# An adaLN mixture-of-experts kernel: a branch hint ahead of the code behind the expert blocks, one product fewer at its start, and the last tile's output in two halves

## The chip, the cores and the metric

The kernel runs on one core of a Trainium2 chip. The metric is the device time of one execution in microseconds; three executions of the kernel before gave 560.17, 560.28 and 561.66 us, with a median of 560.28 us. One further execution was taken under the hardware profiler, and all rows quoted below come from it. Its own device time is 562.46 us, of which the span from the first to the last instruction is 560.6 us.

The engines are named as the profile names them: PE is the matrix engine (PEld are its weight loads), DVE the vector engine, ACT the scalar engine, POOL the GpSimd engine, SP the engine that here only issues DMAs. A letter q behind a name (PEldq, SPq) marks an engine's sequencer, the part that fetches instructions, waits on semaphores and takes branches. L1157 is line 1157 of the kernel's source before the change.

## What is computed

There are 4 batches of 512 rows with 512 columns, in float32. A conditioning layer comes first, then a mixture-of-experts feed-forward layer with 32 experts, 4 of them for each row and at most 512 slots in each expert, and a shared expert beside it. Cut to its core:

```
q_emb = relu(cond @ W3 + b3)
hidden = relu(((512 * x + sum_rows(x)) * q_emb) @ W2 + b2)          # per batch
h = rmsnorm(hidden) * norm_w
scores = softmax(h @ gate_w.T);  top 4 experts, their weights scaled to sum 1
for each expert e, its rows in order, the first 512 of them:        # C = 512
    routed[row] += weight * ((silu(rows @ w13_gate) * (rows @ w13_up)) @ w2[e])
shared = (silu(h @ shared_gate) * (h @ shared_up)) @ shared_down
out = x + hidden + routed + shared
```

A row past an expert's 512 slots is not simply left out by the reference: its index is clipped when the results are read back, so that it receives the result of the expert's last slot, times its own weight. The kernel keeps these "rows of last slots" apart, as is told below.

## The kernel before

The kernel records every operation through a small layer (`op`, line 113): each operation goes to the end of its engine's list, and the layer works out which semaphores it has to wait for from the tiles that it reads and writes. So the order of the Python calls is the order on each engine, and an engine never takes an operation ahead of one that waits.

**The stages.** First the conditioning layer, the gate and the sorting of rows into experts (to about 124 us). Then a long run of blocks: a block is two units of 64 rows that belong to one expert each, and for each the rows are gathered, multiplied by the two weight matrices of their expert, and added into a buffer in DRAM by POOL's scattering DMAs (L1108). How many blocks there are depends on the data, between 16 (`NMIN`) and 80 (`NMAX`); here there are 61. The code of all 80 blocks is written out one behind the other, and ahead of each block from the sixteenth on every engine but SP compares the block's number with the count and either goes on or branches away (L1385).

**The endings.** The branch goes to one of 65 pieces of code, `ending(i)`, one for each possible count: it finishes the one or two blocks still in flight and does a part of the shared expert of batch 1 in between: on PE two halves of a product into `TX[1]` (L880), the transposes and the second product of the last block (L541, L1180), and then `s_half(1, 1, sg_sb, TX[0])`, four products into the bank `TX[0]` (L548). Each ending closes with an unconditional branch (L1393) to code that is there once on each engine, called the rest here (`PE_rest` and so on). In memory the 80 blocks come first, then the 65 endings in order, then the rest.

**The rest** is the shared expert of batches 1, 0, 2 and 3 (batch 0's was computed in front of the blocks) and the sum of all parts. Its order on PE, as recorded:

- `s_half(1, 1, su_sb, GU[1])`: four products (L548); the first waits until ACT and DVE have closed their endings
- four transposes of `over`, the weights of the rows past the slots, into `D[0]` (L541); ACT copies them to `overT` (L1346)
- `down(j)` for the tiles 1, 2, 3, 0 of batch 1 (L1319): two products each, from `t_act` and `sd_sb` into the bank `BK[j]`, where BK is `[D[0], D[1], TA[0], TA[1]]`; they wait for DVE's product of silu and up (`s_mult`, L897)
- `products(2, 0)`: the gate half into `TX[0]`, the up half into `TX[1]`; ACT's silu (L894), DVE's product (L897)
- the rows of last slots: two tiles `lrow[0]` and `lrow[1]` of 32 rows and 512 columns, read from the two DRAM buffers, are multiplied by `copies`, a matrix that repeats the 32 rows four times, and summed in the bank `GU[1]`; ACT copies the sum to `lrows` (L1353)
- then for batches 1, 0, 2 and 3 in turn the shared expert's products, `past(b, ...)` (L1312: four products of 32 rows that add the rows of last slots) and `down`, and for each tile `result(t)`: DVE adds the bank to the sums in `y_sb` (L1330) and SP writes the tile of 128 rows and 512 columns to the output.

SP reads the sums back at the start of the rest (`yin`, L1288: `lrow[0]`, `lrow[1]`, then eight loads of 1 MB), when all scattering DMAs have landed, and POOL adds the two halves of the sums in place (`both`, L1326), four tiles for each batch in the order 1, 0, 2, 3. Two of the lines that the change moves:

```
    op("PE", matmuls([(GU[1][:], copies[:].rearrange("e t f -> e (t f)"), lrow[i][:]) for i in range(2)]),
       r=[copies[:], lrow[0][:], lrow[1][:]], w=[GU[1][:]])
```

Of the kernel before, what the change touches and what calls it, by code (L numbers as in the profile page):

```python
# [11 lines left out]
ALU = mybir.AluOpType  # L12
AX = mybir.AxisListType

P = 128
# [9 lines left out]
class Program:  # L25
# [87 lines left out]
    def op(self, eng, fn, r=(), w=(), lane=None, signal=True, also=(), key=None):  # L113
        need = {}

        def depend(token):
            key, val = token
            need[key] = max(need.get(key, 0), val)

        for token in also:  # L120
            depend(token)
        for x in r:
            for c in self.cells(x):
                if c in self.writer:
                    t = self.writer[c]
                    if not (eng == "PE" and self.owner[t[0]] == "PE"):
                        depend(t)
        for x in w:
            for c in self.cells(x):
                if c in self.writer:  # L130
                    t = self.writer[c]
                    if not (eng == "PE" and self.owner[t[0]] == "PE"):
                        depend(t)
                for t in self.readers.get(c, {}).items():
                    if not (eng == "PE" and self.owner[t[0]] == "PE"):
                        depend(t)
        if lane is not None:
            ring = self.lanes[lane]
            key = ring[self.lane_next[lane]]
            self.lane_next[lane] = (self.lane_next[lane] + 1) % len(ring)  # L140
            if self.count[key]:
                depend((key, self.count[key]))
            self.count[key] += 16
            token, step = (key, self.count[key]), 16
        elif signal:
            key = key or self.own[eng]
            self.count[key] += 1
            token, step = (key, self.count[key]), 1
        else:
            token, step = None, 0  # L150
        waits = self.learn(eng, need)
        if token:
            self.seen[token] = dict(self.known[eng])
            for x in r:
                for c in self.cells(x):
                    self.readers.setdefault(c, {})[token[0]] = token[1]
            for x in w:
                for c in self.cells(x):
                    self.writer[c] = token
                    self.readers.pop(c, None)  # L160
        else:
            assert not w
        self.out[eng].append((waits, fn, token and token[0], step))
        return token
# [43 lines left out]
def adaln_moe_kernel(nc, stack, x, xt, cond, W3, b3, W2, b2, norm_w, gate_w, wx, sg, su, sd, out):  # L208
    B, S, H = x.shape
    Q = cond.shape[1]  # L210
    E = gate_w.shape[0]
# [4 lines left out]
    NT = T // P  # L216
    TB = S // P
# [23 lines left out]
    op = k.op  # L241
# [4 lines left out]
    out_rows = out.rearrange("b (t p) h -> (b t) p h", p=P)  # L246
# [16 lines left out]
    sg_sb = keep("sg_sb", [P, HC, I], F32)  # L263
    su_sb = keep("su_sb", [P, HC, I], F32)
    sd_sb = keep("sd_sb", [P, IC, H], F32)
# [9 lines left out]
    last = keep("last", [P, 2, NCOL], F32)  # L275
# [110 lines left out]
    t_act = k.sbuf("t_act", [P, IC, S], F32, k.place[hT[0].name][1])  # L386
    t_silu = [k.sbuf(f"t_silu{i}", [P, S], F32, at) for i, at in enumerate((after_up2, k.place[hT[0].name][1] + 4096))]
    y_sb = [k.sbuf(f"y{i}", [P, NT, H], F32, ring_at + i * NT * H * 4) for i in range(2)]
    overT = k.sbuf("overT", [P, B, P], F32, ring_at + 2 * NT * H * 4)
    lrow = [k.sbuf(f"lrow{i}", [E, H], F32, ring_at + (2 * NT + 1 + i) * H * 4) for i in range(2)]  # L390
    lrows = k.sbuf("lrows", [P, H], F32, ring_at + (2 * NT + 3) * H * 4)
    copies = k.sbuf("copies", [E, TB, E], F32, ring_at + (2 * NT + 4) * H * 4)
    assert 2 * NT + 5 <= NBUF * WROW // H

    TX = [k.bank(f"TX{i}", i) for i in range(2)]
    GU = [k.bank(f"GU{i}", 2 + i) for i in range(2)]
# [17 lines left out]
    def dma(eng, out_ap, in_ap, lane, r=(), w=()):  # L414
        return op(eng, lambda e: e.dma_start(out=out_ap, in_=in_ap, allow_slow_non_contiguous=True), r=r, w=w, lane=lane)
# [129 lines left out]
    def matmuls(terms):  # L545
        def fn(e):
            for n, (o, lt, rh) in enumerate(terms):
                last = e.matmul(o, lhsT=lt, rhs=rh, start=(n == 0), stop=(n == len(terms) - 1))  # L548
            return last
        return fn  # L550
# [20 lines left out]
    for c in range(QC):  # L571
        op("PE", transposes([(TA[0][:, c * 8 : c * 8 + B], cond_sb[:, c * P : (c + 1) * P], B)]),
           r=[cond_sb[:], ident[:]], w=[TA[0][:]])
# [4 lines left out]
    for c in range(HC):  # L578
        bank = (TX + GU)[c]
        op("PE", matmuls([(bank[:, 0:B], W3_sb[:, kc, c * P : (c + 1) * P], condT[:, kc, :]) for kc in range(QC)]),  # L580
           r=[W3_sb[:], condT[:]], w=[bank[:]])
# [236 lines left out]
    for t in range(NT):  # L818

        g, i = divmod(t - 5, TB)  # L820
# [29 lines left out]
        b, i = divmod(t, TB)  # L850
# [38 lines left out]
    def s_half(b, i, w_sb, pg, key=None):  # L889
        op("PE", matmuls([(pg[:], w_sb[:, c, i * P : (i + 1) * P], hT[b][:, c, :]) for c in range(HC)]),  # L890
           r=[w_sb[:]] + [("hT", b * TB + j) for j in range(TB)], w=[pg[:]], key=key)
# [22 lines left out]
    for e in range(FREE):  # L914
# [22 lines left out]
       r=[cumj[:], ones[:]], w=[TA[1][:]])  # L937
# [6 lines left out]
       w=[active[:]])  # L944
# [4 lines left out]
       r=[ranks[:], before[:], till[:], active[:]], w=[TA[1][:]])  # L949
    op("PE", matmuls([(TA[0][0:1, 4 * NCOL : 4 * NCOL + E], active[:, i : i + 1], upto[:]) for i in range(2)]),  # L950
       r=[active[:], upto[:]], w=[TA[0][:]])
# [13 lines left out]
    for i in range(2):  # L965
        op("DVE", lambda e, i=i: e.tensor_scalar(place[i][:], iota_bk[:], rank[:, i : i + 1], None, ALU.is_equal),
           r=[iota_bk[:], rank[:]], w=[place[i][:]])
    op("DVE", lambda e: e.tensor_tensor(places12[:], place[0][:], place[1][:], ALU.add), r=[place[0][:], place[1][:]],
       w=[places12[:]])
    for t in (12, 13):  # L970
# [9 lines left out]
       r=[scol[:], units], w=[TA[0][:]])  # L980
    op("PE", lambda e: e.matmul(TA[0][0:1, 2 * NCOL : 4 * NCOL], lhsT=ecol[:], rhs=units, start=True, stop=True),
       r=[ecol[:], units], w=[TA[0][:]])
# [21 lines left out]
    for t in range(12, NT):  # L1004
# [11 lines left out]
       r=[empty[:], spare[:], GU[0][:]], w=[idxf[:]])  # L1016
# [14 lines left out]
       r=[needs[:]], w=[tab[:]])  # L1031
# [6 lines left out]
       w=[rel[:]])  # L1038
# [261 lines left out]
    def products(b, i, gate=True):  # L1300
        if gate:
            s_half(b, i, sg_sb, (TX if i == 0 else GU)[0])
        s_half(b, i, su_sb, (TX if i == 0 else GU)[1])
        s_silu_of((TX if i == 0 else GU)[0], t_silu[i][:])
        s_mult(t_silu[i][:], (TX if i == 0 else GU)[1], t_act[:, i, :])

    BK = [D[0], D[1], TA[0], TA[1]]

    def past(b, start, stop):

        for j in range(TB):
            op("PE", lambda e, j=j: e.matmul(BK[j][:], lhsT=overT[j * E : (j + 1) * E, b, :],  # L1312
                                             rhs=lrows[j * E : (j + 1) * E, :], start=start, stop=stop),
               r=[overT[:], lrows[:]], w=[BK[j][:]])

    def down(j, start, stop):
        def fn(e):
            for i in range(IC):
                last = e.matmul(BK[j][:], lhsT=t_act[:, i, j * P : (j + 1) * P], rhs=sd_sb[:, i, :],  # L1319
                                start=start and i == 0, stop=stop and i == IC - 1)  # L1320
            return last
        op("PE", fn, r=[t_act[:], sd_sb[:]], w=[BK[j][:]])

    def both(t):
        a, b = y_sb[0][:, t, :], y_sb[1][:, t, :]
        op("POOL", lambda e: e.tensor_tensor(a, a, b, ALU.add), r=[a, b], w=[a])  # L1326

    def result(t):
        a, po = y_sb[0][:, t, :], BK[t % TB]
        op("DVE", lambda e: e.tensor_tensor(a, a, po[:], ALU.add), r=[a, po[:]], w=[a])  # L1330
        dma("SP", out_rows[t], a, "ost", r=[a])

    for b in order:
        sums_in(b)
# [7 lines left out]
       w=[copies[:]])  # L1342
    for g in range(B):
        op("PE", transposes([(D[0][:, g * P : (g + 1) * P], over[:, g * TB : (g + 1) * TB, :].rearrange("p t e -> p (t e)"),
                              P)]), r=[over[:], ident[:]], w=[D[0][:]])
    op("ACT", lambda e: e.copy(overT[:], D[0][:].rearrange("p (b t) -> p b t", b=B)), r=[D[0][:]], w=[overT[:]])  # L1346
    for j in (1, 2, 3, 0):
        down(j, True, False)
    products(2, 0)

    op("PE", matmuls([(GU[1][:], copies[:].rearrange("e t f -> e (t f)"), lrow[i][:]) for i in range(2)]),
       r=[copies[:], lrow[0][:], lrow[1][:]], w=[GU[1][:]])
    op("ACT", lambda e: e.copy(lrows[:], GU[1][:]), r=[GU[1][:]], w=[lrows[:]])  # L1353
    s_half(2, 1, sg_sb, GU[0])
    past(1, False, True)
    for j in range(TB):
        result(TB + j)
# [8 lines left out]
        result(2 * TB + j)  # L1366
    products(3, 0, False)
    products(3, 1)
    past(3, True, False)
    for j in range(TB):  # L1370
        down(j, False, True)
        result(3 * TB + j)
    k.wait("SP", k.lane_tokens("ost"))


    def writer(eng):
        def fn(e):
            k.emit(e, before_loop[eng])
            if eng != "SP":
                n = k.reg["n" + eng]  # L1380
                root, parents = nc.cur_bb, {}
                for i in range(NMAX):
                    if i >= NMIN:
                        parents[i] = nc.cur_bb
                        e.br_lt(n, i + 1, on_true=f"{eng}_end{i}", on_false=f"{eng}_blk{i}")  # L1385
                        nc.switch_bb(f"{eng}_blk{i}", parent=parents[i])
                    k.emit(e, bodies[i][eng])
                parents[NMAX] = nc.cur_bb
                e.br(f"{eng}_end{NMAX}")
                for i in range(NMIN, NMAX + 1):  # L1390
                    nc.switch_bb(f"{eng}_end{i}", parent=parents[i])
                    k.emit(e, endings[i][eng])
                    e.br(f"{eng}_rest")  # L1393
                nc.switch_bb(f"{eng}_rest", parent=root)
            k.emit(e, after_loop[eng])
        return fn
# [45 lines left out]
```

## Time and profile before

| what | value |
|---|---|
| three executions | 560.17, 560.28, 561.66 us |
| the profiled execution | 562.46 us |
| its span | 560.6 us |
| PE busy | 549.7 us, 98% of the span, 2518 products |
| DVE, ACT, POOL busy | 287.2, 220.8, 287.4 us |
| the 61 blocks, up to the branch to the ending | about 124 to 483 us |
| the ending on PE | 483.9 to 493.3 us |
| the rest on PE | 495.5 to 557.3 us |
| the last tile: DVE's sum, then its DMA | 557.40 us, 558.12 us |

How to read it: a group of instructions on one engine is shown with its start, its length, its line, what it writes and reads, and how often it occurs; a float32 product of 512 columns shows as two matrix instructions, each started 0.43 us after the one before when PE is kept supplied, so four products are "x8". Idle time ahead of a group stands in brackets with what ended it; "issue" says that no semaphore in the profile accounts for it. The mean clock granted to PE is shown as a share of full speed.

### The profile page before, as it was taken

How to read it: one execution, taken by the hardware profiler on the slowest of the kernel's cores; microseconds unless marked ns; L12 is line 12 of the kernel's file. 1: busy time of each engine (PE TensorE's matmuls, PEld its weight loads, DVE VectorE, ACT ScalarE, POOL GpSimd, SP SyncE). 2: the span in 40 equal slices, each digit the busy share in tenths (PEclk: the TensorE clock that was granted, in tenths of full speed). 3: DMA queues.
4: the chain of work that ended last, by engine and by line, in shares of the span. 5: the costliest groups of instructions: out<-in, count | busy, mean ns of one | idle time of the engine just before them, and what ended most of it. 6: DMA issues, size and time to landing. Idle time of an engine off the chain costs nothing.

```text
span 560.6 us, 7813 instructions
## 1 busy us (share of the span) xinstructions
PE 549.7 (98%) x2518; PEld 237.1 (42%) x2518; DVE 287.2 (51%) x807; ACT 220.8 (39%) x428; POOL 287.4 (51%) x237
## 2 busy tenths in 40 slices
PE   8999999999999999999999999999999999989997
PEld 5455665443433333433334433334333334334342
DVE  3569998956455444555444554444554445210422
ACT  3648666823334433434333344333344334300000
POOL 1102200235766666576667776756766766415800
PEclk9999999999999999999999999999999999989999
DMA  8886888956686968797997889989999655439921
GB/s 300 286 324 239 283 337 279 360 174 190 111 198 112 238 147 197 197 238 180 250 260 185 236 242 267 238 230 251 222 250 248 113 103 92 67 56 381 343 77 75
DMA packets 49198, 120.21 MB, mean 214 GB/s; under 512 B 8404, under 2 KB 9432, under 8 KB 48056
## 3 DMA queue, kind: packets, MB, share of 16 engines
q1 hardware_dynamic: 32896, 83.24, 43.9%
q0 software_dynamic: 15040, 34.39, 31.2%
q10 hardware_dynamic: 1208, 1.92, 1.0%
q8 instruction: 26, 0.43, 0.3%
q14 instruction: 28, 0.23, 0.1%
HBM read 89.36 MB, written 34.36 MB: 221 GB/s over the span
## 4 chain that ended last, share of the span: by engine, by line
PE 92%; DVE 3%; ACT 2%; issue 1%; DMA 1%; POOL 0%; SPq 0%; DVEq 0%; ACTq 0%
PE GU L1157 37%; PE D L1180 20%; PE D L548 7%; PE TX L541 5%; PE TX L548 5%; PE GU L548 4%; PE TA L541 4%; PE D L1319 2%; PE TA L1319 2%; PE TX L880 2%; PE TA L548 1%; DMA z<-in_xt_dram 1%; PE D L598 1%; PE D L558 1%; PE D L1312 1%
## 5 line engine op out<-in xcount | busy, mean ns | idle before, releaser
L1108 POOL DMA_INDIRECT y_rows<-eo,sidx x122 | 180.4, 1479 | 102.8 <-DMA y_rows<-eo,sidx 34.7
L1157 PE MATMUL GU<-ring,xT 128*64 x488 | 214.5, 592 | 0.6 <-issue 0.6
L1157 PE MATMUL GU<-up,xT 128*64 128x512 f32 x488 | 214.5, 592 | 0.0
L1157 PEld LDWEIGHTS GU<-ring,xT 128*64 128x64 f32 x488 | 66.8, 137 | 139.4 <-issue 139.4
L1165 DVE TENSOR_TENSOR act<-silu,GU 128x256 f32<-128x256 f32 x61 | 25.7, 422 | 176.3 <-ACT silu L1164 143.4
L1180 PE MATMUL D<-ring,actT 128*64 x244 | 111.3, 599 | 0.2 <-issue 0.2
L1180 PE MATMUL D<-down,actT 128*64 128x512 f32 x244 | 111.3, 599 | 0.0
L1100 POOL DMA_INDIRECT rows<-h_rows,idx x66 | 70.5, 1068 | 33.6 <-issue 13.1
L1164 ACT ACTIVATE silu<-GU 128x256 f32<-128x256 f32 x61 | 23.5, 385 | 147.6 <-PE GU L1157 147.6
L1157 PEld LDWEIGHTS GU<-up,xT 128*64 128x64 f32 x488 | 66.8, 137 | 0.0
L1068 ACT COPY up<-ring 128x1024 f32 x62 | 64.3, 1037 | 5.8 <-DVE up L1068 5.5
L1184 ACT ACTIVATE eo<-D,wrow 128x512 f32<-128x512 f32 x61 | 41.9, 687 | 51.5 <-PE D L1180 42.7
L1180 PEld LDWEIGHTS D<-ring,actT 128*64 128x64 f32 x244 | 30.9, 136 | 58.0 <-issue 58.0
L548 PE MATMUL D<-W_sb,z 128*128 128x512 f32 x120 | 54.3, 595 | 0.2 <-POOL z L563 0.2
L1068 DVE COPY up<-ring 128x1024 f32 x62 | 44.7, 721 | 0.8 <-issue 0.8
L1068 DVE COPY down<-ring 128x1024 f32 x62 | 42.7, 714 | 0.1
L1096 DVE COPY xT<-TX 128x512 f32<-128x512 f32 x62 | 40.0, 686 | 4.4 <-issue 2.0
L563 POOL TENSOR_SCALAR z<-z,vs,q_sb 128x512 f32<-128x512 f32 x12 | 9.8, 816 | 55.7 <-ACT junk L554 55.6
L541 PE MATMUL TX<-ident,rows 128*128 128x128 f32 x248 | 32.3, 273 | 0.0
L1171 ACT COPY actT<-TA 128x256 f32<-128x256 f32 x61 | 22.8, 373 | 24.1 <-PE TA L541 18.1
L548 PEld LDWEIGHTS D<-W_sb,z 128*128 128x128 f32 x120 | 21.7, 190 | 22.4 <-issue 22.0
L1180 PEld LDWEIGHTS D<-down,actT 128*64 128x64 f32 x244 | 30.9, 136 | 0.0
(207 smaller groups left out, 561.2 us busy)
## 6 DMA issues: line engine op xcount, KB each, us to landing
ring<-in_L_ffn_w_dram SPq DMA_DIRECT2D x96, 384.0 KB
ring<-in_L_ffn_w_dram SPq DMA_DIRECT2D x8, 1536.0 KB
y<-y_rows SPq DMA_DIRECT2D x8, 1024.0 KB, 13.4
h_rows<-h SPq DMA_DIRECT2D x16, 256.0 KB, 4.5
y_rows<-hid SPq DMA_DIRECT2D x16, 256.0 KB, 4.1
out_dram<-y SPq DMA_DIRECT2D x16, 256.0 KB, 2.3
z<-in_xt_dram SPq DMA_DIRECT2D x14, 256.0 KB, 5.3
y_rows<-eo,sidx POOLq DMA_INDIRECT x122
```

The lines of the kernel that those rows point to most:

```text
L541: last = e.transpose(o, i, ident[:n, :n])
L548: last = e.matmul(o, lhsT=lt, rhs=rh, start=(n == 0), stop=(n == len(terms) - 1))
L1068: return e.copy(dst, src) if eng == "ACT" else e.tensor_copy(dst, src)
L1096: return op("DVE", lambda e: e.tensor_copy(xt[:], pt[:].rearrange("p (c t) -> p c t", c=HC)), r=[pt[:]], w=[xt[:]])
L1100: op("POOL", lambda e: e.indirect_dma_start(out=r[:], out_offset=None, in_=h_dram, in_offset=bass.IndirectOffsetOnAxis(ap=idx[:, i : i + 1 ...
L1108: op("POOL", lambda e, o=o, y=y, at=at: e.indirect_dma_start(out=y, out_offset=bass.IndirectOffsetOnAxis(ap=at, axis=0), in_=o, in_offset= ...
L1157: last = e.matmul(pg[h * U : (h + 1) * U, :], lhsT=xt[:, c, h * U : (h + 1) * U], rhs=w, start=(c == 0), stop=(c == HC - 1))
L1164: op("ACT", lambda e: e.activation(s, pg[:, 0:I], AF.Silu), r=[pg[:]], w=[s])
L1165: op("DVE", lambda e: e.tensor_tensor(a, s, pg[:, I : 2 * I], ALU.mult), r=[s, pg[:]], w=[a])
L1171: op("ACT", lambda e: e.copy(at[:], pt[:, 0 : IC * P].rearrange("p (c t) -> p c t", c=IC)), r=[pt[:]], w=[at[:]])
L1180: last = e.matmul(po[h * U : (h + 1) * U, :], lhsT=at[:, c, h * U : (h + 1) * U], rhs=w2, start=(c == 0), stop=(c == IC - 1))
L1184: op("ACT", lambda e: e.activation(o, po[:], AF.Copy, scale=w), r=[po[:], w], w=[o])
```

## The change

Four edits are made, all in or behind the endings.

- Each ending on PE begins with a branch hint: the place is marked at the ending's first instruction, and the unconditional branch at its end is named as the hinted one. No other engine gets one. In the instruction lists this is one instruction more in each of the 65 endings on PE.
- In the rest, the gate half of `products(2, 0)` is recorded ahead of the four `down`, so on PE it stands between the transposes of `over` and `down`.
- The two products with `copies` become one: DVE adds `lrow[1]` to `lrow[0]` first. In DVE's list the sum stands behind the product of silu and up of `products(2, 0)`, and reads two tiles in SBUF of 32 rows and 512 columns.
- The last tile of batch 3 is computed in two halves of 256 columns, the left one in `TA[1]` as before, the right one in `TX[0]`: `past`, `down`, DVE's sum and the output's DMA occur twice for it, each on 256 columns. SP issues 17 output DMAs in place of 16.

The instruction lists of the two kernels differ in nothing else.

```diff
-    def past(b, start, stop):
+    def past(b, start, stop, tiles=range(TB)):
-        for j in range(TB):
+        for j in tiles:
             op("PE", lambda e, j=j: e.matmul(BK[j][:], lhsT=overT[j * E : (j + 1) * E, b, :],
...
-    def down(j, start, stop):
+    def down(j, start, stop, f0=0, f1=H, bank=None):
+        bank = bank or BK[j]
         def fn(e):
             for i in range(IC):
-                last = e.matmul(BK[j][:], lhsT=t_act[:, i, j * P : (j + 1) * P], rhs=sd_sb[:, i, :],
+                last = e.matmul(bank[:, f0:f1], lhsT=t_act[:, i, j * P : (j + 1) * P], rhs=sd_sb[:, i, f0:f1],
                                 start=start and i == 0, stop=stop and i == IC - 1)
...
-    def result(t):
-        a, po = y_sb[0][:, t, :], BK[t % TB]
-        op("DVE", lambda e: e.tensor_tensor(a, a, po[:], ALU.add), r=[a, po[:]], w=[a])
-        dma("SP", out_rows[t], a, "ost", r=[a])
+    def result(t, f0=0, f1=H, bank=None):
+        a, po = y_sb[0][:, t, f0:f1], (bank or BK[t % TB])[:, f0:f1]
+        op("DVE", lambda e: e.tensor_tensor(a, a, po, ALU.add), r=[a, po], w=[a])
+        dma("SP", out_rows[t][:, f0:f1], a, "ost", r=[a])
...
+    s_half(2, 0, sg_sb, TX[0])
     for j in (1, 2, 3, 0):
         down(j, True, False)
-    products(2, 0)
-
-    op("PE", matmuls([(GU[1][:], copies[:].rearrange("e t f -> e (t f)"), lrow[i][:]) for i in range(2)]),
-       r=[copies[:], lrow[0][:], lrow[1][:]], w=[GU[1][:]])
+    products(2, 0, False)
+
+    op("DVE", lambda e: e.tensor_tensor(lrow[0][:], lrow[0][:], lrow[1][:], ALU.add), r=[lrow[0][:], lrow[1][:]],
+       w=[lrow[0][:]])
+    op("PE", matmuls([(GU[1][:], copies[:].rearrange("e t f -> e (t f)"), lrow[0][:])]),
+       r=[copies[:], lrow[0][:]], w=[GU[1][:]])
...
-    past(3, True, False)
-    for j in range(TB):
+    halves = ((0, H // 2, BK[TB - 1]), (H // 2, H, TX[0]))
+    past(3, True, False, range(TB - 1))
+    for f0, f1, bank in halves:
+        op("PE", lambda e, f0=f0, f1=f1, bank=bank: e.matmul(
+            bank[:, f0:f1], lhsT=overT[(TB - 1) * E : TB * E, 3, :], rhs=lrows[(TB - 1) * E : TB * E, f0:f1],
+            start=True, stop=False), r=[overT[:], lrows[:]], w=[bank[:]])
+    for j in range(TB - 1):
         down(j, False, True)
         result(3 * TB + j)
+    for f0, f1, bank in halves:
+        down(TB - 1, False, True, f0, f1, bank)
+        result(NT - 1, f0, f1, bank)
...
                 for i in range(NMIN, NMAX + 1):
                     nc.switch_bb(f"{eng}_end{i}", parent=parents[i])
+                    hint = e.mark_branch_hint_location() if eng == "PE" else None
                     k.emit(e, endings[i][eng])
-                    e.br(f"{eng}_rest")
+                    to_rest = e.br(f"{eng}_rest")
+                    if hint is not None:
+                        to_rest.branch_hint(hint)
```

## The prediction

> **What bounds the kernel now.** I read the busy shares first, then the chain of waits from 482 us on, because the change touches nothing before that.
>
> ```profile
> PE 549.7 (98%) x2518; PEld 237.1 (42%) x2518; DVE 287.2 (51%) x807; ACT 220.8 (39%) x428; POOL 287.4 (51%) x237
> ...
> 489.70 3.63 PE TX L548 x8
> 493.33 2.21 issue
> 495.54 5.40 PE GU L548 x8
> ...
> 501.06 0.68 DVE t_act L897
> 501.74 0.04 issue
> 501.78 1.98 PE D L1319 x4
> ...
> 508.92 6.87 PE TX L548 x16
> 515.78 5.54 PE GU L548 x12
> ...
> 553.86 3.45 PE TA L1319 x8
> ...
> 557.40 0.69 DVE y L1330
> ```
>
> PE sets the time. Behind the blocks its chain has three blemishes: 2.21 us of nothing at the start of the rest, a first group that takes 5.40 us where every other "x8" takes 3.4 to 3.7, and a wait for DVE's product at 501. Next I read the windows, for the clock, and the branch's own record.
>
> ```profile
> 493.50:496.90 3.40, 1.36 (x3) 0.68 (x4) 0.62 (x1) 0.46 (x1) 0.31 (x1) 1.00 0.38 51
> 496.90:500.30 3.40, 3.40 (x5) 1.31 (x4) 0.00 (x0) 0.00 (x0) 0.00 (x0) 0.50 0.02 5
> ...
> 555.00:558.40 3.40, 2.30 (x6) 0.75 (x4) 1.37 (x2) 0.00 (x0) 0.00 (x0) 1.00 0.41 154
> 558.40:560.60 2.20, 0.00 (x0) 0.00 (x0) 0.00 (x0) 0.00 (x0) 0.00 (x0) 1.00 0.32 119
> ...
> L1393 PEldq COMPARE_BRANCH  x1: 3992/3992/3992, 487.8 to 487.8; - x1
> ```
>
> The columns of the windows are length, busy time of PE, PEld, DVE, ACT, POOL, PE's granted clock, DMA share and GB/s. After a stretch in which PE was busy 1.36 of 3.40 us the clock was halved for one stretch: that is the 5.40. After 2.30 of 3.40 it was not.
>
> The branch to the rest took PE's sequencer 3.99 us, from 487.78 to 491.77. But PE still had products queued until 493.07, so **the branch itself is hidden**. In the trace's records of transfers, PE's code arrives in loads of 16,384 bytes: one runs from 489.41 to 490.35 (the branch's target), the next from 492.52 to 494.23. The rest's first instruction, a wait, is recorded at 491.84, its second at 495.53. So I read the gap thus: the rest begins at the very end of a load, and PE runs dry on the next one. A pair of blocks has 135 PE instructions in 11.91 us, and loads come every 23.0 us ((478.04 - 109.95) / 16), so a load holds about 260 instructions.
>
> **The change part by part**, against the profiled execution.
>
> *Hint, and the place of the rest.* 65 endings grow by one instruction, so the rest moves 65 instructions on, out of the end of a load, with some 195 of it left in that load: over 15 us of work, which covers the next load. With that, or with a hint that fetches early, PE goes on when the last product is issued: the eighth starts at 489.63 + 7 x 0.43 = 492.64, the next is due at 493.07 and came at 495.54. Saved: 2.4 us; 0 if the rest again meets a load's end. The cover is the 4 x 2 x 0.43 = 3.4 us of the ending's last product; without it the branch's 4.0 us would show. The hint stands where PE is already idle (483.00 to 483.91), so its price counts in full: at least the 0.05 us of another sequencer instruction (the regops of L1180 took 46 to 53 ns), at most the 4.0 us of the branch if it waits for the fetch. A hint has only to issue a request, like the first: 0.05.
>
> *The clock.* Without the gap its drop goes: 5.40 - 3.70 = 1.7 us; 0 if the new stall below brings one back.
>
> *The gate half ahead of `down`.* PE waits 0.41 us for DVE's product at 501.37; now 3.4 us of products stand there and cover it: 0.4 saved. ACT's silu comes earlier too, and nothing waits for it.
>
> *One product fewer, one sum on DVE.* Two matrix instructions go: 2 x 0.43 = 0.86 us saved. But the sum stands in DVE's list behind `products(2, 0)`'s product, and this one waits for the up half, which PE issues directly ahead of the `copies` product. Where PE went on at 515.71, it now waits: DVE's product starts at 515.89, the sum can start 0.60 later (DVE's sums of L1330 in a row: two in 1.29) and takes 0.70 (between 0.69 of L1330 and 0.75 of L611, 128x512 with both inputs in SBUF), and PE follows 0.07 later (501.73 to 501.78 for the same step): 517.26, that is 1.55 late. The sum also reads two SBUF tiles while POOL adds the halves of the sums:
>
> ```profile
> 100.69 0.97 DVE L733 SCALAR_TENSOR_TENSOR blk<-idf,blk 128x16 f32<-128x16 f32 x1
> ...
> 100.59 1.04 POOL L762 TENSOR_TENSOR over<-over,kept 128x384 f32<-128x384 f32 x1
> ...
> 510.72 4.93 POOL L1326 TENSOR_TENSOR y<-y,y 128x512 f32<-128x512 f32 x4 [16.90 <-DMA y<-y_rows]
> 516.14 4.93 POOL L1326 TENSOR_TENSOR y<-y,y 128x512 f32<-128x512 f32 x4 [0.49 <-DMA y<-y_rows]
> ```
>
> L733 with two SBUF inputs needs 0.17 us alone and took 0.97, to the end of POOL's instruction; L737 at 46.98 lost 0.38 in the same way, and then ran between two of POOL's. So the sum waits 0 to 1.27 us (one instruction of L1326); I take 0.5, between the losses 0.38 and 0.80. Together 1.55 + 0.5 - 0.86 = +1.2, from +0.6 to +2.0. Behind the `copies` product stand all further products of PE and ACT's copy to `lrows`. The loads of `lrow` land 2.2 us after 501.4, long before. On DVE `result(4)` stands behind, at 522.5 less about 2 to 4 us, while POOL's sums for it end at 515.65 and at most 0.7 later.
>
> [...]
>
> *A new clock drop.* The stall leaves PE idle about 1.55 + 0.5 + 0.1 = 2.1 us, up to 62% of 3.4, against the 60% that brought a drop and the 32% that did not: 0 to +1.7. [...]
>
> *The last tile.* DVE's last sum falls from 0.69 (L1330) to 0.42 (L1165, 128x256): 0.27. Its DMA moves half: 64 KB (lrow) land in 2.2 us, 256 KB in 2.3, so 0.1, at most 0.34 (half of a queue's 8 packets of 0.085 us). PE works as long: `past`'s fourth runs beside the other three in its own rows, and a weight load of 0.19 fits under 0.21 of a half product. SP's one issue more (0.33) stands 0.86 ahead of the last. 0.4 saved, 0.1 to 0.6.
>
> **Sum** without clock: -2.4 + 0.05 - 0.4 + 1.2 - 0.4 = -1.95. The profiled execution, 562.46, is 2.2 us above the median of 560.28, more than one drop; so I can't tell whether the median holds a drop. Where the drop is in both kernels or in neither, the median goes to 560.28 - 1.95 = **558.3**.
>
> **The cases.**
> - *Forecast, 46%*: as summed, 558.3; own range 557.4 to 559.3.
> - *The old drop goes, none comes, 28%*: -1.7 more, 556.6. For it: a gap of 2.47 us fills over half of some 3.4 us stretch at most alignments. Against it: the new stall is nearly as long.
> - *Only the new stall brings a drop, 12%*: 560.0.
> - *The change doesn't do what it says, 8%*: the branch was hidden already, and the rest's place gains nothing because another load's end lies as badly: the gap stays, 558.3 + 2.4 = 560.7.
> - *Slower, 6%*: the hint waits for its fetch at the ending's first instruction, where no product is queued. Price 4.0 us, and a drop of 1.7 behind 4.9 us of idle PE: 558.3 + 4.0 + 1.7 = 564.0. For it: the branch's record, which does wait. From a price of 2.0 on the kernel is no faster.
>
> 0.3% is 1.7 us here, about what a measurement can tell: faster is below 558.6, slower above 562.0. About two thirds of the forecast (0.30) and the second case (0.28) with a little of the others give 0.60 for faster; the slower case with the upper ends of the two before it 0.09; same 0.31. The range 556.0 to 560.6 takes the first three cases and the unknowns of the sum.
>
> **What would show it.** PE's branch at the ending's end takes far below 3.99 us, and the rest's first product follows the ending's last at once, at full clock. On the `copies` product stands an idle time of PE of 1.6 to 2.9 us, put down to DVE's sum; the sum shows above 0.75 us if POOL holds it. The wait ahead of `down` is gone. DVE's last sum takes 0.42. I am wrong if PE is idle at the ending's first product for more than 0.95 us, if the gap before the rest stays, or if the sum ends ahead of the up half.

## The result, and the profile after

Over 16 runs of each, the changed kernel has a median of 559.46 us (557.17 to 561.53) and the kernel before 560.37 us (559.50 to 563.16). The ratio is 0.9969, with a 95% interval from 0.9952 to 0.9986: about 1.7 us less by the ratio, 0.9 by the medians. The profiled execution of the changed kernel took 560.65 us, its span 558.8; the one before took 562.46, its span 560.6.

The changed kernel's runs fall into two groups by the mean granted clock that each run reports. Six runs at 1.000 have a median of 558.28 us, ten at 0.994 to 0.997 one of 560.07. One stretch of 3.41 us at half clock is 1.7 us lost, or 0.3% of the mean clock, and that is the distance of the two groups (1.8 us). Of the kernel before, 34 later runs were taken on three chips; five of them stand at 0.996 or 0.997 (two of 21, three of 11, none of two) and the rest at 0.999 or 1.000. The mean clock does not say where a stretch at half clock lies. In three of the profiles below that show 0.997 (without the hint near a load's end, the later hint, the early sum without the hint) it lies at 8.4 to 11.8 us, in the first stage, and none lies between there and the last product.

First the busy shares of the changed kernel, from the top of its page:

```profile
PE 549.1 (98%) x2522; PEld 238.4 (43%) x2522; DVE 287.9 (52%) x809; ACT 220.7 (40%) x428; POOL 287.1 (51%) x237
```

PE sets the time as it did (the counts are of matrix instructions, two for each float32 product). Next its chain of waits from the ending's last product on; the columns are start, length and what ran.

```profile
490.27 3.63 PE TX L548 x8
493.90 3.43 PE GU L548 x8
...
508.07 3.45 PE TX L548 x8
...
512.22 1.56 DVE lrow L1354
...
513.82 6.45 PE GU L548 x10
...
555.39 0.88 PE TX L1321 x4
556.27 0.02 issue
556.29 0.42 DVE y L1332
```

All three blemishes of the profile before are gone: the rest's first product starts at 493.90, the moment the ending's last ends, it takes 3.43 us where it took 5.40, and no wait for DVE stands at 501. A new one has come in their place. PE ends its last block of products at 511.52 and goes on at 513.82, behind DVE's sum of the two `lrow` tiles, and the group that follows takes 6.45 us. Ten such instructions at full clock take 4.68 (the same group in an experiment below). The windows, with the columns that the prediction names, show why:

```profile
512.00:515.40 3.40, 1.58 (x3) 0.59 (x4) 1.76 (x2) 0.42 (x1) 3.40 (x3) 1.00 1.05 389
515.40:518.90 3.50, 3.50 (x6) 1.43 (x5) 0.00 (x0) 0.16 (x1) 3.47 (x4) 0.51 1.05 388
518.90:522.30 3.40, 3.40 (x15) 1.16 (x14) 0.87 (x2) 0.60 (x1) 2.91 (x3) 1.00 1.05 387
```

PE was busy for 1.58 of 3.40 us, and in the next stretch it got half its clock. The drop lasted 3.41 us and then went away. The sum itself, from the timeline and, for POOL, from the group of its instructions (shortest, median and longest in ns):

```profile
511.61 0.69 DVE L897 TENSOR_TENSOR t_act<-t_silu,TX 128x512 f32<-128x512 f32 x1 [10.17 <-PE TX L548]
512.22 1.55 DVE L1354 TENSOR_TENSOR lrow<-lrow,lrow 32x512 f32<-32x512 f32 x1
513.82 1.12 PE L548 MATMUL GU<-lrow,copies 32*128 32x512 f32 x2 [2.32 <-DVE lrow L1354]
```

```profile
L1328 POOL TENSOR_TENSOR y<-y,y x16: 1257/1265/1712, 510.7 to 530.6; 128x512 f32<-128x512 f32 x16
```

The sum took 1.55 us from 512.22 to 513.76. One of POOL's adds ran from 511.96 to 513.22, and the sum, which takes 0.68 us alone (an experiment below), ended 0.54 us behind it. So I read it as held until about the end of that add. The next of POOL's adds, from 513.18 on, was the long one, 1.71 us instead of 1.26. So each held the other once. Last, the branch to the rest and the hint on PE's sequencer, as groups (the same three times in ns):

```profile
L1408 PEldq COMPARE_BRANCH  x1: 4152/4152/4152, 488.3 to 488.3; - x1
...
L1406 PEldq BRANCH_PREFETCH_HINT  x1: 50/50/50, 484.4 to 484.4; - x1
```

The hint cost 50 ns and the branch took 4.15 us, a little more than before (3.99). It is hidden by the products queued ahead of it, which ran until 493.90 while the branch ended at 492.50, and it was not made shorter.

**Where the time went**, profile against profile, on PE (from start to start in the timeline, where the rest's first product after the change starts at 493.73):

| stretch | before, us | after, us | difference |
|---|---|---|---|
| ending's first product to the rest's first product | 11.63 | 9.24 | -2.39 |
| rest's first product to the `copies` product | 20.17 | 20.09 | -0.08 |
| `copies` product to the past slots of batch 3 | 33.38 | 34.21 | +0.83 |
| PE's last product to the end of the span | 3.3 | 2.6 | -0.7 |

The second line holds 5.40 - 3.43 = 1.97 and 0.41 saved, and 2.32 of new stall. The third holds a clock drop, 6.45 - 4.68 = 1.77, and the two matrix instructions of one product fewer, 0.86. The four sum to -2.4. The ending itself began 0.58 us later in the profile after, in code that the change does not touch; with that the spans differ by 1.8.

### The profile page after: what moved, and what is told of

It is laid out like the page before. It is cut to its first block, busy times and chain, and to the rows that moved or that the text cites. A ratio compares the mean times of both kernels' runs of the same rounds, so it can differ in the third digit from the quotient of the medians.

```text
span 558.8 us, 7827 instructions
## 1 busy us (share of the span) xinstructions
PE 549.1 (98%) x2522; PEld 238.4 (43%) x2522; DVE 287.9 (52%) x809; ACT 220.7 (40%) x428; POOL 287.1 (51%) x237
## 4 chain that ended last, share of the span: by engine, by line
PE 95%; DVE 3%; ACT 1%; issue 1%; DVEq 0%
PE GU L1157 38%; PE D L1180 20%; PE D L548 9%; PE TX L548 5%; PE TX L541 5%; PE TA L541 5%; PE GU L548 4%; PE D L1321 2%; PE TX L880 2%; PE TA L1321 2%; PE TA L548 1%; PE D L598 1%; PE D L558 1%; PE D L1312 1%; PE D L880 1%
## 5 line engine op out<-in xcount | busy, mean ns | idle before, releaser
L1100 POOL DMA_INDIRECT rows<-h_rows,idx x66 | 69.2, 1049 | 33.7 <-issue 11.6
```

The costliest lines, as they stand in the source:

```text
L1100: op("POOL", lambda e: e.indirect_dma_start(out=r[:], out_offset=None, in_=h_dram, in_offset=bass.IndirectOffsetOnAxis(ap=idx[:, i : i + 1 ...
```

## The experiments

Twelve kernels, one of them the kernel before once more, were run in three groups, each group beside runs of the kernel before on the same chip: its median was 560.46 us (21 runs) for the first four, 562.02 (one run) for the next four, 561.66 (11 runs) for the last four. "Dead" instructions below are transposes that stand in PE's code behind the last ending and are never reached, since the data takes another ending. They only move the rest's place in PE's code.

**Place alone.** The kernel before, with 64 dead instructions and no hint:

```diff
                     k.emit(e, endings[i][eng])
+                    if eng == "PE" and i == NMAX:
+                        for _ in range(32):
+                            e.transpose(TX[0][:, 0:P], ident[:], ident[:])
                     e.br(f"{eng}_rest")
```

> The kernel before, with 32 transposes (64 PE instructions) written into the ending for 80 blocks, which is never entered here, so that the rest lies 64 instructions further on; no hint and none of the other edits. Theory of the place: the gap of 2.2 us ahead of the rest goes although the branch still takes 4.0 us, no clock drop follows, and the time falls by 2.4 to 4.1 us from some 560.4, to 556.3 to 558.0. Theory of the hint: without a hint nothing changes, 560.4, and the gap of 2.2 us stays.

Measured: 558.71 us (557.69 to 560.83, 9 runs), ratio 0.9973, 0.9961 to 0.9986. Its chain of waits at the rest's beginning:

```profile
489.80 3.63 PE TX L548 x8
493.43 3.43 PE GU L548 x8
```

The gap and the drop behind it are gone without any hint, and the gain is as large as that of the whole change (ratio 0.9973 against 0.9969). The branch took 3.67 us and was hidden as well. PE's code loads came at 489.07 and 492.3 and then not before 525.73.

**The hint alone, with the rest's old place.** The kernel before with the change's hints, and 190 dead instructions. With the 65 of the hints that is 255, so that the rest stands one instruction ahead of its old place, counted in loads of 256 instructions (the prediction worked out about 260 from the rows; the runs near a load's end, below, fit 256: there 252 dead instructions move the gap by four, and 252 + 4 = 256):

```diff
+                    hint = e.mark_branch_hint_location() if eng == "PE" else None
                     k.emit(e, endings[i][eng])
-                    e.br(f"{eng}_rest")
+                    if eng == "PE" and i == NMAX:
+                        for _ in range(95):
+                            e.transpose(TX[0][:, 0:P], ident[:], ident[:])
+                    to_rest = e.br(f"{eng}_rest")
+                    if hint is not None:
+                        to_rest.branch_hint(hint)
```

> The kernel before with the branch hint in every ending, and 95 transposes (190 PE instructions) in the ending for 80 blocks, which is never entered here: with the 65 hints the rest moves by 255 of about 256 instructions, so it stands as near to the end of a code load as before. Theory of the place: the gap of 2.2 us and the 4.0 us of the branch stay, 560.4 within 0.8. Theory of the hint: the branch falls far below 4.0 us, the gap goes, 556.3 to 558.0.

Measured: 559.03 us (558.05 to 559.52, 7 runs), ratio 0.9970, 0.9959 to 0.9981. The branch took 3.56 us, and yet the gap was gone. This spoke against "the hint does nothing". The loads gave the clue: 489.68 and 492.9, and the next only at 531.89. In the kernel before, whose rest begins at a load's end, the third load came at 497.16, 4.64 us behind the second. So either one instruction of difference had moved the rest to the beginning of a load, or the hint had part in it. The runs that follow tell which.

**Near a load's end, without and with the hint, and the kernel before again.** As above, with 252 dead instructions and no hint, and with the hints and 186 dead ones (251 in all). In its old place the rest has one instruction left in its load (its wait, recorded at 491.84, while the second came at 495.53), so these stand 5 and 6 instructions ahead of a load's end. The kernel before was profiled a second time beside them.

```diff
-                        for _ in range(95):
+                        for _ in range(126):
```
```diff
-                        for _ in range(95):
+                        for _ in range(93):
```

> The kernel before, unchanged, in another profiled execution. If a gap of 2.2 us ahead of the rest is typical, it shows again between 2.0 and 2.4. If it was long because the second code load took 1.72 us where most take about 1.05, it shows at 1.4 to 1.8, and with it the clock drop may be missing.

> The kernel before with 126 transposes (252 PE instructions) in the ending for 80 blocks, which is never entered here, and no hint: the rest begins some 4 instructions earlier in a code load than before, again close to its end. Theory of the place: as before, three loads around the branch, and a gap ahead of the rest's first or second product of 1 to 2.2 us. If what counts is something other than the place, the gap is gone as in the run with 64 instructions.

> The same place within an instruction as the run without hints near the end of a load, but with the 65 hints and 93 transposes (186 PE instructions) in the ending that is never entered. If a hint does nothing, this run shows the same gap of 1 to 2.2 us as the one without hints. If the gap is gone here and there in the other, the hint (or where the loader puts a hinted target) is what removes it. In either case the branch takes 3.4 to 4.2 us if the hint fetches nothing early, and under 1 us if it does.

Measured, one run each: 560.93, 558.94 and 558.22 us. The chains of waits, the kernel before first, then without and with the hint:

```profile
490.68 3.63 PE TX L548 x8
494.31 1.43 issue
495.74 3.70 PE GU L548 x8
```

```profile
489.49 3.63 PE TX L548 x8
493.12 0.86 PE GU L548 x2
493.98 0.62 issue
494.60 2.84 PE GU L548 x6
```

```profile
489.64 3.63 PE TX L548 x8
493.27 3.43 PE GU L548 x8
```

Four instructions (two pairs of a weight load and a matrix instruction) further from the load's end, exactly two matrix instructions run ahead of the gap, and the gap is shorter by 1.43 - 0.62 = 0.81, about the time of these two (0.86). That is the place theory to the instruction: the rest runs to the end of its load and waits for the next. Here that load ran from 492.10 to 493.17, and the products went on 1.43 us behind its end; in the two profiles of the kernel before it was 1.30 and 1.39. With the hint and one instruction further still, there is no gap, and no third load until 531.95: the rest stands at the beginning of a load of its own. The branch is as long in all three: 3.74, 3.63 and, with the hint,

```profile
L1397 PEldq COMPARE_BRANCH  x1: 3878/3878/3878, 487.7 to 487.7; - x1
```

The second profile of the kernel before matters for sizes too: its gap is 1.43 us where the first profile had 2.21, and no drop follows (3.70). The load it waits for took 1.09 us here and 1.72 there.

**How near.** The same with 180 and 172 dead instructions, 245 and 237 in all, which puts the rest 12 and 20 instructions ahead of a load's end:

```diff
-                        for _ in range(95):
+                        for _ in range(90):
```
```diff
-                        for _ in range(95):
+                        for _ in range(86):
```

> The kernel before with 65 hints and 90 transposes (180 instructions) in the ending that is never entered: by the count the rest begins 12 instructions ahead of the end of a code load. If a target with a hint is left where it is, a second load is met some 12 instructions on and a third is fetched at about 496, as in the unhinted run near the end. If a hinted target is moved to the beginning of a load, there are two loads around the branch and the next only at about 532. No gap over 0.3 us in either case.

> The same with 86 transposes (172 instructions): 20 ahead of the end. If only a target a few instructions short of a load's end is moved, here the third load shows at about 495 to 497 and the count is confirmed; if there are two loads and the next at about 530, the count of instructions is off or every hinted target is moved.

Measured, one run each: 557.12 and 559.19 us, the branch 3.13 and 3.84, no gap in either. At 12 the loads come at 487.63, 490.75 and 529.86: again a load of its own. At 20 they come at 490.11, 493.28 and 496.98: a third load follows 3.70 us behind the second, as in the kernel before (4.64), and the products that these 20 instructions had queued cover it. So the count is right. The hinted target stood at the beginning of a fresh load where by the count it would have been 2, 6 or 12 instructions ahead of the end of one, and not at 20. An unhinted one 5 ahead of the end did not. What moved the hinted ones, no run shows. In the changed kernel, where the rest is 65 instructions from its old place, this has no part: with the early sum, which follows, the third load came 32.6 us behind the rest's first product with the hint and 33.2 us without, and where the rest was moved it came 37.7 to 38.7 us behind.

**The sum ahead of the products.** The changed kernel, with DVE's sum recorded directly behind `copies`:

```diff
        w=[copies[:]])
+    op("DVE", lambda e: e.tensor_tensor(lrow[0][:], lrow[0][:], lrow[1][:], ALU.add), r=[lrow[0][:], lrow[1][:]],
+       w=[lrow[0][:]])
...
-    op("DVE", lambda e: e.tensor_tensor(lrow[0][:], lrow[0][:], lrow[1][:], ALU.add), r=[lrow[0][:], lrow[1][:]],
-       w=[lrow[0][:]])
     op("PE", matmuls([(GU[1][:], copies[:].rearrange("e t f -> e (t f)"), lrow[0][:])]),
```

> The changed kernel with DVE's sum of the rows of last slots recorded right behind the copies, ahead of the product of silu and up of batch 2. Theory of the stall: the sum then runs about 505 us, as soon as its two loads have landed and some 6 us before POOL's sums begin, takes 0.6 to 0.75 us in place of 1.55, and PE's idle time of some 2.1 us ahead of the copies product goes, with the clock drop that it brings in about six of ten executions: 559.5 - 2.1 - 1.0 = 556.4, with no execution's clock below full. Rival (the stall is cover for something else that ends as late, POOL's sums or the loads): 559.5 within 0.6, the idle time turns up at the next products.

Measured: 557.00 us (556.63 to 560.32, 10 runs), ratio 0.9950, 0.9934 to 0.9965; two of the ten runs have a clock of 0.997, and they are the two slowest (559.36 and 560.32). The sum in its timeline, and the chain at the `copies` product:

```profile
504.31 0.68 DVE L1345 TENSOR_TENSOR lrow<-lrow,lrow 32x512 f32<-32x512 f32 x1 [2.64 <-DMA lrow<-y_rows]
```

```profile
508.29 3.43 PE TX L548 x8
511.73 4.68 PE GU L548 x10
```

The same sum takes 0.68 us there, ahead of POOL's adds, and nothing stands between the products. The 2.32 us of stall and the drop were the price of the sum's place in DVE's list.

**Both products, no sum.** The changed kernel with the `copies` product on both tiles again:

```diff
-    op("DVE", lambda e: e.tensor_tensor(lrow[0][:], lrow[0][:], lrow[1][:], ALU.add), r=[lrow[0][:], lrow[1][:]],
-       w=[lrow[0][:]])
-    op("PE", matmuls([(GU[1][:], copies[:].rearrange("e t f -> e (t f)"), lrow[0][:])]),
-       r=[copies[:], lrow[0][:]], w=[GU[1][:]])
+    op("PE", matmuls([(GU[1][:], copies[:].rearrange("e t f -> e (t f)"), lrow[i][:]) for i in range(2)]),
+       r=[copies[:], lrow[0][:], lrow[1][:]], w=[GU[1][:]])
```

> The changed kernel with the two products with copies as before and no sum on DVE. Theory of the stall: the idle time ahead of the products goes and 0.86 us of products come back, 559.5 - 2.1 + 0.86 - 1.0 = 557.3, so this edit alone made the changed kernel slower by about 2.2 us. Rival (one product fewer is worth its 0.86 us and the stall is small beside it): 560.3.

Measured: 557.85 us (557.31 to 558.62, 5 runs, all at a clock of 1.000), ratio 0.9952, 0.9939 to 0.9966. No stall, and the branch took 3.39. It stands 0.85 us above the early sum by the medians, and in the chains its group at the `copies` product takes 5.54 us against 4.68: the price of the two matrix instructions of one product (0.86). The ratios, 0.9952 and 0.9950, do not separate the two kernels; the chains do. So this part of the change, as it stands, loses, and the same edit a few lines earlier gains.

**A later hint.** The early sum, with the hint put into the ending behind its second pair of products:

```diff
+        k.raw("PE", lambda e: k.reg.__setitem__(("hint", i), e.mark_branch_hint_location()))
         for n in left:
             b_down(n)
...
-                    hint = e.mark_branch_hint_location() if eng == "PE" else None
                     k.emit(e, endings[i][eng])
+                    hint = k.reg["hint", i] if eng == "PE" else None
```

> The changed kernel with the early sum, and the hint not at the ending's first instruction but behind the second pair of products of its first half (in front of the last block's second product), about 1 us later for the sequencer, when the code load that follows the branch to the ending is under way or over. If a hint is dropped because that load is still to come, the branch now falls under 2 us; if hints do nothing here, it stays at 3.4 to 4.2 us. The time is that of the early sum, 557.0 within 1.5, in both cases, since the branch is hidden.

Measured, one run: 556.29 us; the branch took 3.61. The hint ran at 484.24, near the same time as in the changed kernel (484.38), because PE's sequencer ran far ahead of its products: those that stand ahead of this hint ran on PE until 488.12. So this run did not put the hint later in time, and it leaves open whether another moment would let it fetch.

**The early sum without the hint.** No hints; 64 dead instructions keep the rest's place.

```diff
-                    hint = e.mark_branch_hint_location() if eng == "PE" else None
                     k.emit(e, endings[i][eng])
-                    to_rest = e.br(f"{eng}_rest")
-                    if hint is not None:
-                        to_rest.branch_hint(hint)
+                    if eng == "PE" and i == NMAX:
+                        for _ in range(32):
+                            e.transpose(TX[0][:, 0:P], ident[:], ident[:])
+                    e.br(f"{eng}_rest")
```

> The early sum without any hint, the rest moved by 64 instructions of the ending that is never entered. If the hint earns nothing of its own, 557.0 within 0.5, the branch takes 3.4 to 4.2 us as with it. If the hint earns something, slower by over 0.5.

Measured: 556.14 us (555.36 to 558.02, 6 runs), ratio 0.9908, 0.9884 to 0.9933. This is the fastest version that was run; it lies 5.5 us under the kernel before by the medians, 3.8 to 6.5 by the interval. No gap, and the branch took 3.63. Because the early sum with the hint ran on another chip (ratio 0.9950), the two do not tell what the hint is worth within a few tenths of a per cent; that the kernel needs no hint they do tell.

**The last tile in one piece.** The early sum with the hint, its last tile as before the change:

```diff
-    halves = ((0, H // 2, BK[TB - 1]), (H // 2, H, TX[0]))
-    past(3, True, False, range(TB - 1))
...
-    for j in range(TB - 1):
+    past(3, True, False)
+    for j in range(TB):
         down(j, False, True)
         result(3 * TB + j)
-    for f0, f1, bank in halves:
-        down(TB - 1, False, True, f0, f1, bank)
-        result(NT - 1, f0, f1, bank)
```

> The early sum with the last tile computed and written as a whole, as before. If the halves are worth what the end of the two profiles shows (3.24 us from PE's last product to the end before, 2.51 behind the change), this run is 0.7 us slower than the early sum: 557.7 against 557.0. If the halves only move work, 557.0.

Measured: 557.82 us (556.47 to 558.63, 6 runs), ratio 0.9927, 0.9905 to 0.9950. Ends of the two chains, in one piece and (from the early sum) in halves:

```profile
553.35 0.03 issue
553.44 0.69 DVE y L1332
```

```profile
551.53 0.88 PE TX L1321 x4
552.43 0.42 DVE y L1332
```

From PE's last product to the end of the span it takes 3.31 us in one piece and 2.58 in halves: 0.73. Of it 0.27 is DVE's shorter sum. Another 0.07 lies between PE's last product and DVE's sum (0.11 against 0.04), and 0.2 shows as the store's time from issue to landing (a median of 2.0 us for 256 KB in the kernel before, 1.8 for 128 KB in the changed one); the other 0.19 no view assigns. The medians of this kernel and of the early sum without the hint, on the same chip, differ by 1.7 us, which is more than the ending can be: the profile in one piece also waited longer ahead of the ending's first product, 1.82 us against 0.42. So the size is taken from the stretch.

That wait differs over the profiles. It is 0.28 to 0.91 us in the five without hints (0.42 in the median) and 0.44 to 1.82 in the nine with them (0.87). It goes with the branch from the blocks to the ending, which took 3.4 to 4.0 us in the five and 3.4 to 4.7 in the nine. That branch runs ahead of the hint, but the hints also lengthen the endings that lie in front of this one and so move its place. Whether the hints cost about 0.4 us in this way or the difference is chance, no run here separates.

## Why the prediction was right, step by step

The forecast was 558.3, within 556.0 to 560.6; the median is 559.46: faster, by about as much as the prediction said that a measurement can tell. The runs without a drop have 558.28, so the forecast's own case, "the drop is in both kernels or in neither", met what it described. But most runs were not of that case.

- **What bounds it, and the gap.** Right: the rest began at a load's end, the place removed the gap, and the branch stayed hidden. The three runs near a load's end show it, and the place alone shows it. Mis-sized: -2.4 is what the profiled execution lost. That execution waited for a load of 1.72 us, while the second profile lost 1.43 with a load of 1.09. The place alone gains 1.75 by the medians, so a term between -1.4 and -1.8 would have fitted the median.
- **The hint.** That it has only to issue a request was an assumption of mine. The term of 0.05 was right for the hint itself (50 ns); whether moving the endings costs more is open (above). The place I could show to be enough; that the hint fetches early I had left open, and it does not. The branch took 3.1 to 4.2 us in nine kernels with the hint and 3.6 to 4.0 in five profiles without, and the target's load began behind the branch's start in all fourteen. My sign "PE's branch at the ending's end takes far below 3.99 us" failed, at 4.15. It could not have told the place from the hint in any case, since a branch that is hidden may be of any length. The slower case, a hint that waits for its fetch, fell. The cover of the branch was larger than the 3.4 us that the prediction counted: PE had products until 493.90, 5.55 us behind the branch's start.
- **The gate half ahead of `down`.** -0.4 was right: the wait of 0.41 us is gone.
- **One product fewer, one sum on DVE.** The mechanism was right in each part: the sum stands behind the up half's product, starts 0.61 us after it (0.60 was taken), and is held by one of POOL's instructions. Held 0.87 us (1.55 - 0.68), where I took 0.5 within 0 to 1.27. The net came to 2.32 - 0.86 = +1.46 against +1.2, inside the range of +0.6 to +2.0. POOL's next add took 1.71 us against 1.26.
- **The old clock drop.** Its term was 0 to -1.7, and the case in which it goes and no other comes had 28%. It is hardly there to go: of the 34 later runs of the kernel before, five show the mean clock of a drop, wherever it lay, and the second profile has none. The profiled execution was one of the few with one. The clue lay in the times, 562.46 against a median of 560.28, and I declined to decide from it.
- **The new clock drop.** This is the step that failed. "Only the new stall brings a drop, 12%" is what happened in the profiled execution, and ten of 16 runs have a mean clock that fits; their median of 560.07 is the 560.0 of that case. I had 2.1 us of idle PE "up to 62% of 3.4" against the 60% that brought a drop, and gave it 12% because the old gap was taken to bring one as often. But the gap is typically 1.4 us and the new stall 2.3. The mean clock does not tell where a drop lies, so that all ten fell behind the stall was not seen; without the stall none of five runs (both products), two of ten (early sum) and two of six (early sum without the hint, whose profile has its drop in the first stage) show one. The yardstick failed too: the share of idle time does not decide. Stretches of 3.41 us with PE busy for 1.50 us (the hint near a load's end, from 551.56), 1.73 us (the hint alone, from 552.22) and 1.88 us (the last tile in one piece, from 484.14) were not followed by half clock, and with 1.63 us behind the change, counted over the 3.41 us up to the drop, one was. In that stretch two of the four matrix instructions have 32 rows in place of 128, which may count; no run varies it.
- **The last tile.** -0.4 (to -0.6) was too small: -0.7 in the stretch, and 0.73 in the experiment. DVE's part was right, 0.69 to 0.42. Sized wrong was what follows it, the store, taken at 0.1 by bytes and at 0.34 at most: from the end of DVE's sum to the end of the span it is 2.51 us in one piece and 2.12 in halves, 0.39 less. The 0.07 ahead of DVE's sum was not in the term at all.

Taken together the typical gap is about 1 us smaller than taken, the end 0.3 better, and the stall with its frequent drop takes back most of what the place brings. Right in the sum, and partly by luck: the errors have opposite signs.

**What stays open.** Why the hint does not shorten the branch, and whether it would from another place in time; what moves a hinted target that is near a load's end; the hint's own worth or price below some 0.5%; and what, beside PE's busy time, decides whether a stall brings a clock drop.

## What to carry to other kernels

Where code is reached by a branch, look at where in its load the target lies: here a target in the last instructions of a load (one left in the kernel before, five without the hint near a load's end) stalled PE for 0.62 to 2.21 us behind the branch, and 64 instructions that never run, put ahead of it, moved it at no price that showed (558.71 us against 560.46). A small operation that the bounding engine will wait for belongs at the head of the other engine's list, as soon as its inputs are there; behind the last dependent step the sum cost here its own 0.68 us, 0.87 us held by POOL's add and, in the profiled execution, a clock drop (3.41 us at half clock). Profile a kernel twice before pricing a stall: one execution showed 2.21 us and a drop, the next 1.43 and none.

## What the runs showed of the hardware

- **A stall of 2.32 us was followed by half of PE's clock.** 2.32 us without a product, in a stretch in which PE was busy 1.58 of 3.40 us, brought 3.41 us at half clock, and 1.36 of 3.40, with a stall of 2.21, did so before, again for 3.41. No bound by busy time comes out of the profiles: 1.50, 1.73 and 1.88 us of 3.41 brought none, and neither did 2.30 of 3.40 at the end of the kernel before, but 2.30 of 3.41 in the first stage (from 4.97 us, without the hint near a load's end) did.
- **The branch to the rest held PE's sequencer for 3.1 to 4.2 us** in the fourteen profiles. Its target's load began behind the branch's start (1.63 us behind it in the kernel before, 1.31 in the changed one) and itself took only some 0.9 to 1.4 us (0.94 and 1.41). The next load in order came 3.1 to 3.6 us after the first. The branch cost nothing while enough products were queued ahead: in the changed kernel it took 4.15 us and they lasted until 5.55 us behind its start.
- **The prefetch hint on PE cost 50 ns and did not shorten the branch** (3.1 to 4.2 us with it, 3.6 to 4.0 without). But with the hint, targets that by the count would have stood 2, 6 and 12 instructions ahead of a load's end began a load of their own, as the third load shows, which came only at 529.86 to 531.95; at 20 it came at 496.98.
- **DVE's sum of the two `lrow` tiles, which met POOL's back-to-back adds, got in between two of them**, at about the end of the one that ran (1.55 us instead of 0.68), and held the next, 1.71 us instead of 1.26.
